# Eleven prefetched adapter tiles in a row behind the thirteen in place, the convolution's working memory released in two parts, and the first chunk's remaining rows begun an adapter sooner

## Chip, cores and metric

The kernel runs on one core of a Trainium2 chip. The metric is the device time of one execution in microseconds (us). The kernel before was run three times: 2236.38, 2232.4 and 2238.17, median 2236.38. The profiled execution took 2235.61, with a span of 2234.0 from the first to the last profiled instruction, so 1.6 us lie around the span.

## What is computed

The reference takes `x` of shape (32, 64, 1024): 32 samples of 64 rows. Four layers follow, each added to its input:

```python
x = x + _L0(x, ...)   # a state-space kernel K(64 rows x 1024), convolved with each row, plus D*x, masked by length
x = x + _L1(x, ids1, w1)   # w1[ids1[b]]: one 1024 x 1024 float32 matrix for each sample
x = x + _L2(x, ids2, w2)   # the same with another table and other ids
x = x + _L3(x, ...)   # gated feed-forward 1024 -> 2752 -> 1024, silu(gate) * up, with rank-16 adapters by sample
```

Everything is float32. L1 and L2 are the "adapters" here: each of the 32 samples needs a matrix of 4 MB of its own in each of the two layers, which is read from device memory for that sample alone.

## The kernel before

**Chunks.** The samples are handled in four chunks (`NCK`) of eight (`BC`). The convolution (`convolution`, called at L289) is computed for all chunks at once; the first chunk's result goes into `xs[0]` and the others' into the device buffer `cd`. Then chunk 0 goes through its 16 adapters (two layers by eight samples) and its feed-forward; the adapters of a later chunk are taken between pieces of the feed-forward of the chunk before it.

**An adapter's tiles.** A matrix is cut into eight tiles of 128 x 1024 float32 (512 KB, `KT` = 8). `adapter(layer, b)` (L252) takes tile after tile from the iterator `stream` and multiplies; `adapter_part` (L229) does one of the two halves (`s` = 0, 1) of the sample's 64 rows. When the eight tiles are through, VectorE (DVE) transposes the PSUM bank into the tile `y` (L263) and adds it to `x` (L265). The 128 tiles of chunk 0 are numbered k = 0 to 127 here, in the order in which TensorE (PE) needs them; `layers` (L155) gives the order of the adapters.

**Where tiles lie.** SyncE's queue (SP) issues all their loads, in the program's order. Nine places rotate (`wpool`, `ROTATING` = 9): a load into one waits until PE has read the tile that lies there. Besides there are places that hold one tile each, loaded while the convolution runs ("own" places, list `early`): 16 in `epool`, four in the half of `xpool` that chunk 1 will use, five ("late") where the convolution's tables lay, nine ("last") where its transfers lay. That makes 34; `own` (L184) says which k lie in them: 2, 5, 8, ... 101, every third. Before the adapters begin, 34 own tiles and the first nine others (k = 0, 1, 3, 4, 6, 7, 9, 10, 12) are on their way. `fetch(n)` issues the next n of these 43 loads in the order of k, at points written out by hand: L2072, L2021 (`MID`), L2074, then two a period, then `LATE` at L1997 and the rest at L1982.

**What the convolution frees, and when.** `g0` lives until `first.close()`, `gb` (transfers `uf`, `hk`, state of even groups, small tiles) until `filling.close()` at L1980, `s1` until `making.close()`. The last of the eight groups (`NG_`) is only multiplied with its taps (`direct`) after the carried part of the group before it; `filling.close()` stands behind both, so the nine loads into "last" wait for the last `direct`.

**Ahead.** While the convolution's last two groups run, PE does the half s = 0 of the first 13 tiles (`first_sides` L240: all eight of the first adapter, `SECOND_` = 5 of the second) in pieces (`ahead_`). When `xs[0]` is complete, the other half of these 13 follows, and then tile k = 13.

**From the adapters into the feed-forward.** After 12 adapters (`OWN_ENDS`) `first.close()` frees all own places and `g0`, and the pools of the feed-forward (`hpool`, `gpool`, `apool`, `qpool`) take their memory. Then the steps stand in this order (L1224 to L1262): `begin_rest(0)` (the product of one half of the chunk's rows with a weight tile `wr`, which takes a rotating place, L351); the loads of two feed-forward weights (`first_weight`, into `wf0_first` and `act_first`); adapter 13; a part of the feed-forward's moving sums; `begin_rest(1)`; adapter 14; tables of the low-rank part by GpSimd (POOL); `begin_rest(2)`; `begin_products(0)` with the two loaded weights; adapter 15; `begin_products(1)`; adapter 16. `wr0` keeps its rotating place until the feed-forward has used its second half.

**y.** Until `first.close()`, `y` lies in a pool of its own (`ypool`, 2 KB by partition); afterwards in `gpool`.

Of the kernel before, what the change touches and what calls it, by code (L numbers as in the profile page):

```python
# [9 lines left out]
F32 = mybir.dt.float32  # L10
# [9 lines left out]
P = 128  # L20
B, H, L = 32, 64, 1024
NS = 64
KT = L // P
NCK = 4
# [7 lines left out]
MB = 4  # L32
MG = 2
NG = FM // MG
EARLY = 16
OWN_ENDS = 12
LATE = 5
LAST = 9
KS = 5
WARM = 20  # L40
FIRST_ = 11
SECOND_ = 5
MID = 6
ROTATING = 9
HA = 4
# [39 lines left out]
def kernel(  # L85
# [95 lines left out]

    own = {3 * i + 2 for i in range(len(early) + LATE + LAST)}  # L184
    held = {}

    def first_weights():
# [29 lines left out]
        for _ in range(n):  # L217
            next(before, None)

    def places(n):  # L220

        late = n == LATE
        name = "late" if late else "last"
        pool = first.enter_context(
            tc.tile_pool(name=name, bufs=1, side="right" if late else "left")
        )
        for i in range(n):
            early.append(pool.tile([P, L], F32, tag=f"{name}{i}", name=f"{name}{i}"))

# [56 lines left out]
                ALU.add,  # L286
            )

    convolution(tc, cst, consts, xt, xf, ssm, eye, lens, xs[0], cd, ps_tile, fetch, places, (row_ids, rows_now), first, first_sides())  # L289
    for _ in before:  # L290
        pass

# [33 lines left out]
    def take(c):  # L326
# [12 lines left out]

    ypool = [
        first.enter_context(tc.tile_pool(name="ypool", bufs=1, reuse_waits="tile"))
    ]

    def adapters(c):
        for layer, b in layers(c):
# [839 lines left out]
    def begin_rest(i):  # L1187
        wt, ps = rest_tile(i, "first")[0], ps_tile(f"pr{i}_first")
        rest_part(0, wt, ps, 0, TH)
        nc.scalar.copy((rest1, rest2[:, 0], rest2[:, 1])[i][:, :TH], ps[:, :TH])  # L1190
        return wt
# [38 lines left out]
        first_weight(m, 0)  # L1230
    xb, part = first_moving()
    next(layers0)
    part(0, 2)
    begin_rest(1)
    next(layers0)
    tables = [
        columns(ag, 0, KT, "g_0", behind=loads[-1]),
        columns(au, 0, KT, "u_0", ("cu", "lt")),
    ]
    begin_rest(2)  # L1240
    begin_products(0)
    next(layers0)
    part(2, 3)
# [20 lines left out]
def convolution(tc, cst, consts, xt, xf, ssm, eye, lens, x0, cd, ps_tile, fetch, places, rows_now, first, sides):  # L1264
# [12 lines left out]
    with ExitStack() as ctx:  # L1277
        ctx.enter_context(tc.manual_schedule(engines={DVE, ACT, POOL, SP}))
        g0 = first.enter_context(tc.tile_pool(name="g0", bufs=1))
        filling, making = ExitStack(), ExitStack()  # L1280
        gb = filling.enter_context(tc.tile_pool(name="gb", bufs=1))
        s1 = making.enter_context(tc.tile_pool(name="s1", bufs=1, side="right"))
        dram = ctx.enter_context(
            tc.tile_pool(name="kdram", bufs=1, space=bass.MemoryType.DRAM)
# [10 lines left out]
        def load_u(g):  # L1295
            for u in range(PAIRS[g] // 2):
                i = first_unit[g] + u
                ufs[i] = gb.tile([P, HA, NCK, KT * BC], F32, tag="uf", name=f"uf{i}", bufs=4)
                nc.sync.dma_start(ufs[i], xf[:, i * HA : (i + 1) * HA])

        load_u(0)
# [423 lines left out]
        def load_taps(g):  # L1725
            for u in range(PAIRS[g] // 2):
                i = first_unit[g] + u
                hks[i] = gb.tile([P, HA, P], F32, tag="hk", name=f"hk{i}", bufs=2)
                queue = nc.scalar if g == NG_ - 1 else nc.sync
                queue.dma_start(  # L1730
                    hks[i],
                    bass.AP(
                        tensor=kps.tensor,
                        offset=kps[i * HA : i * HA + 1, 1:2].offset,
                        ap=[[1, P], [KROW, HA], [1, P]],
                    ),
                )
# [211 lines left out]
        def period(g):  # L1949


            steps = scan(g + 1) if units(g + 1) else iter(())
            ma, mb = (products(g + 3, u) for u in range(2))
            copies = []

            def turn_next(u):
                copies.append(powers_turned(g + 2, u))

            def copy():
                copies.pop(0)()  # L1960

            first, second = taken(g, 0), taken(g, 1)
            events = [(0, lambda: carried(g, 0))]
            if not units(g + 1):
                for u in range(2):
                    carried(g, u, KS, KT - 1)
                ahead_(SECOND_)
                for c0, c1 in ((0, 1), (1, NCK)):
                    for u in range(2):
                        for f in taken(g, u, c0, c1):  # L1970
                            f()
                return
            if not units(g + 2):

                def ahead():
                    ahead_(3)
                    for u in range(2):
                        direct(g + 1, u)
                    ahead_(3)
                    filling.close()  # L1980
                    places(LAST)
                    fetch(99)  # L1982

                events += [
                    (3, lambda: carried(g, 1)),
                    (3, ahead),
                    *spread(4, (*first, *second)),
                    (3 * KS - 3, lambda: carried(g + 1, 0, 0, KS)),
                    (3 * KS - 3, lambda: carried(g + 1, 1, 0, KS)),
                ]  # L1990
            elif not units(g + 3):

                def close():
                    kernels(g + 2)
                    making.close()
                    places(LATE)
                    fetch(LATE)  # L1997

                events = [
                    (0, lambda: turn_next(0)),  # L2000
                    (0, copy),
                    *events,
                    *spread(1, adds.pop((g + 2, 1))),
                    (3, lambda: carried(g, 1)),
                    (3, close),
                    *spread(3, first[:2]),
                    (4, lambda: inputs(g + 2, 0)),
                    (5, first[2]),
                    (6, lambda: turn_next(1)),
                    (6, copy),  # L2010
                    *spread(6, second),
                    (9, lambda: direct(g + 1, 0)),
                    (9, lambda: inputs(g + 2, 1)),
                    (12, lambda: (direct(g + 1, 1), ahead_(2))),
                ]
            elif g:
                events = [
                    (0, lambda: turn_next(0)),
                    (0, copy),
                    *events,  # L2020
                    *spread(1, adds.pop((g + 2, 1))),  # L2021
                    (3, lambda: carried(g, 1)),
                    *spread(3, first[:2]),
                    (4, lambda: made(ma, 8)),
                    (4, lambda: inputs(g + 2, 0)),
                    (5, first[2]),
                    (6, lambda: turn_next(1)),
                    (6, lambda: made(ma, 3)),
                    (6, copy),
                    *spread(6, second),  # L2030
                    (9, lambda: direct(g + 1, 0)),
                    (9, lambda: made(ma)),
                    (9, lambda: inputs(g + 2, 1)),
                    (9, lambda: made(mb, 3)),
                    (9, lambda: kernels(g + 2)),
                    (10, lambda: adds[g + 3, 0][0]()),
                    (11, lambda: adds.pop((g + 3, 0))[1]()),
                    (12, lambda: made(mb)),
                    (12, lambda: direct(g + 1, 1)),
                ]  # L2040
            else:
                events += [
                    *spread(1, adds.pop((g + 2, 0))),
                    (3, lambda: turn_next(0)),
                    (3, copy),
                    (3, lambda: carried(g, 1)),
                    *spread(3, first[:2]),
                    (4, lambda: made(ma, 8)),
                    (4, lambda: inputs(g + 2, 0)),
                    (5, first[2]),  # L2050
                    *spread(6, adds.pop((g + 2, 1))),
                    (8, lambda: turn_next(1)),
                    (8, lambda: made(ma, 3)),
                    (8, copy),
                    *spread(8, second),
                    (10, lambda: direct(g + 1, 0)),
                    (10, lambda: made(ma)),
                    (10, lambda: inputs(g + 2, 1)),
                    (10, lambda: made(mb, 3)),
                    (10, lambda: kernels(g + 2)),  # L2060
                    (13, lambda: adds[g + 3, 0][0]()),
                    (14, lambda: adds.pop((g + 3, 0))[1]()),
                    (14, lambda: made(mb)),
                    (14, lambda: direct(g + 1, 1)),
                ]
            run(steps, events)
            if units(g + 3):
                load_u(g + 3)
            if units(g + 2):
                load_taps(g + 2)  # L2070

        fetch(FIRST_)  # L2072
        opening()
        fetch(4)  # L2074
        for g in range(NG_):
            period(g)
            if g < NG_ - 4:
                fetch(2)
        rows_now[1]()

# [168 lines left out]
```

## Time and profile before

| | us |
|---|---|
| median of three runs (2232.4 to 2238.17) | 2236.38 |
| the profiled execution | 2235.61 |
| its span | 2234.0 |
| PE busy | 2190.5 (98%) |
| DVE busy | 1369.6 (61%) |
| ACT, POOL busy | 424.2, 207.9 |
| convolution: PE's first matmul to the end of the 13 tiles' second half | 8.4 to 148.3 |
| PE's longest wait for a tile | 148.3 to 155.1 |
| rest of chunk 0's adapters and what is mixed in | 155.1 to 278.5 |
| feed-forward and the later chunks' adapters | 278.5 to 2234.0 |

A row of the profile's timeline of an engine gives the start of a stretch of like instructions, its length, the line of the code, the operands and the number of records, and in brackets how long the engine had been idle and what ended that. PE has two records for each matmul of the code, so a whole tile is 16 records and one half of its rows is 8; "x" at the end counts records. In the profile "pa" is an adapter's PSUM bank, "wa" a tile in a rotating place, and "early", "x_early", "late", "last" are tiles in own places.

### The profile page before, as it was taken

Reading aid. Unit: us, or ns where it says so; the run is one execution under the profiler, and the core shown is the slowest. Engines: PE = TensorE matmul, PEld = TensorE weight load, DVE = VectorE, ACT = ScalarE, POOL = GpSimd, SP = SyncE. Lnnn points to the kernel's source line nnn. Section 1 sums busy time; section 2 is a strip of 40 time slices with the busy share of each in tenths; the row PEclk is TensorE's granted clock in tenths of the full one; section 3 lists DMA queues with packets and bytes.
Section 4 is the critical chain, followed back from the end, with each engine's and each line's share of the span. In section 5 each row is a group of like instructions: output and inputs, shape, how many; then the busy total and the mean of one; then the engine's idle time right before and its main releaser. Section 6 shows DMA issues by size and latency. Waiting matters only on the chain.

```text
span 2234.0 us, 53648 instructions
## 1 busy us (share of the span) xinstructions
PE 2190.5 (98%) x21488; PEld 1811.1 (81%) x21488; DVE 1369.6 (61%) x2995; ACT 424.2 (19%) x1042; POOL 207.9 (9%) x328
## 2 busy tenths in 40 slices
PE   6889999999999999999999999999999999999999
PEld 5756687877787897888689897789678988899998
DVE  8961277675367766466346667466336666576575
ACT  6800121110011121121012212022002212121220
POOL 1010031111011211000000111000000011000000
PEclk9999999999999999999999999999999999999999
DMA  8789998899979558799979848799989938384671
GB/s 313 264 326 408 383 385 304 327 365 358 362 286 362 207 198 306 288 360 362 350 281 367 282 146 321 267 351 364 353 292 360 334 107 290 117 295 177 214 275 42
DMA packets 204683, 656.35 MB, mean 294 GB/s; under 512 B 24066, under 2 KB 40834, under 8 KB 203922
## 3 DMA queue, kind: packets, MB, share of 16 engines
q1 hardware_dynamic: 173122, 565.84, 69.6%
q0 software_dynamic: 23392, 76.07, 9.1%
q10 hardware_dynamic: 7920, 11.01, 1.4%
q8 instruction: 169, 2.77, 0.5%
q14 instruction: 80, 0.66, 0.1%
HBM read 585.66 MB, written 67.17 MB: 292 GB/s over the span
## 4 chain that ended last, share of the span: by engine, by line
PE 85%; DMA 6%; DVE 5%; issue 3%; POOL 0%; ACT 0%; SPq 0%; POOLq 0%; DVEq 0%; ACTq 0%
PE pq L720 30%; PE po L1130 24%; PE pa L234 16%; PE pf L614 6%; DMA wa<-in_w 4%; PE pr L359 3%; PE pe L481 2%; DVE xg L1338 1%; DMA sums<-kept 1%; PE pl_d L452 1%; DVE t L1338 1%; DVE tmp L1338 1%; PE pr_first L359 0%; DVE zs L1338 0%; DMA hk<-kp 0%
## 5 line engine op out<-in xcount | busy, mean ns | idle before, releaser
L234 PE MATMUL pa<-wa,x 128*32 128x256 f32 x7648 | 435.3, 380 | 12.7 <-DMA wa<-in_w 12.4
L720 PE MATMUL pq<-xd,wa 128*128 128x128 f32 x3360 | 414.6, 275 | 0.0
L720 PEld LDWEIGHTS pq<-xd,wa 128*128 128x128 f32 x3360 | 394.6, 192 | 0.1
L234 PEld LDWEIGHTS pa<-wa,x 128*32 128x32 f32 x7648 | 244.8, 110 | 184.4 <-DMA wa<-in_w 21.9
L720 PE MATMUL pq<-xd,wb 128*128 128x128 f32 x2520 | 323.7, 276 | 0.0
L720 PEld LDWEIGHTS pq<-xd,wb 128*128 128x128 f32 x2520 | 300.5, 192 | 3.6
L263 DVE STREAM_TRANSPOSE y<-pa 128x512 f32<-128x512 f32 x64 | 45.9, 717 | 275.8 <-PE pa L234 275.8
L1130 PE MATMUL po<-act,wd 128*128 128x256 f32 x640 | 168.6, 386 | 0.0
L1130 PE MATMUL po<-actd,s 128*128 128x256 f32 x640 | 164.2, 379 | 0.0
L1130 PE MATMUL po<-actd,wd 128*128 128x256 f32 x640 | 164.2, 379 | 0.0
L507 DVE TENSOR_TENSOR s<-wd 128x256 f32<-128x256 f32 x80 | 33.8, 422 | 176.5 <-PE po L1130 176.4
L1130 PEld LDWEIGHTS po<-act,wd 128*128 128x128 f32 x640 | 117.8, 190 | 29.3 <-issue 12.9
L378 POOL DMA_INDIRECT bgu<-in_bgu,rows x44 | 44.7, 1016 | 984.2 <-PE pe L481 827.3
L614 PE MATMUL pf<-xd,wf 128*128 128x256 f32 x576 | 135.5, 381 | 0.0
L1130 PEld LDWEIGHTS po<-actd,s 128*128 128x128 f32 x640 | 121.6, 190 | 16.5
L1130 PEld LDWEIGHTS po<-actd,wd 128*128 128x128 f32 x640 | 121.6, 190 | 16.5
L1162 ACT COPY uo<-po 128x256 f32<-128x256 f32 x48 | 17.9, 373 | 615.0 <-PE po L1130 599.3
L614 PEld LDWEIGHTS pf<-xd,wf 128*128 128x128 f32 x576 | 108.7, 190 | 15.5
L614 PE MATMUL pf<-xd,s 128*128 128x256 f32 x480 | 114.5, 382 | 1.4 <-DVE up L655 0.9
L744 ACT COPY u<-pq 128x256 f32<-128x256 f32 x120 | 41.5, 346 | 366.7 <-PE pq L720 307.3
L614 PEld LDWEIGHTS pf<-xd,s 128*128 128x128 f32 x480 | 90.2, 190 | 17.3 <-DVE up L655 2.8
L749 DVE TENSOR_TENSOR u<-u,u 128x256 f32<-128x256 f32 x120 | 46.5, 388 | 73.2 <-ACT u L746 72.7
(273 smaller groups left out, 2762.4 us busy)
## 6 DMA issues: line engine op xcount, KB each, us to landing
wa<-in_w SPq DMA_DIRECT2D x478, 512.0 KB
wa<-sums SPq DMA_DIRECT2D x210, 512.0 KB
wb<-parts SPq DMA_DIRECT2D x120, 384.0 KB
wd<-in_wd SPq DMA_DIRECT2D x80, 512.0 KB
wb<-in_wq SPq DMA_DIRECT2D x90, 384.0 KB
sums<-kept POOLq DMA_DIRECT2D x30, 1024.0 KB
wf<-in_wu SPq DMA_DIRECT2D x20, 512.0 KB
uf<-in_xf SPq DMA_DIRECT2D x16, 512.0 KB
```

The lines of the kernel that those rows point to most:

```text
L234: nc.tensor.matmul(acc[i * S : (i + 1) * S, s * 256 : (s + 1) * 256], xs[lo // TC][:, kt, lo % TC + s * S : lo % TC + (s + 1) * S], wt[:, ...
L263: nc.vector.transpose(y, acc)
L359: nc.tensor.matmul(ps[:, tokens], wt[:, kt, :], xs[c][:, kt, tokens], start=(kt == 0), stop=(kt == KT - 1),)
L378: nc.gpsimd.indirect_dma_start(out=t, out_offset=None, in_=table, in_offset=bass.IndirectOffsetOnAxis(ap=at_, axis=0),)
L481: nc.tensor.matmul(ps[:, at_ * 2 * H : (at_ + 1) * 2 * H], bt[pair(j), g], tms[table][pair(j)], start=(g == 0), stop=True, skip_group_chec ...
L507: nc.vector.tensor_add(s1, a21, a22)
L614: nc.tensor.matmul(ps, ws[j][:, kt, :], xb[j][:, kt, :], start=start and kt == 0, stop=kt == KH - 1, skip_group_check=True,)
L720: nc.tensor.matmul(ps[:, to * TQ : (to + 1) * TQ], w[i][:, k, :], xb[:, j, SLOT[i], k, :], start=start and k == 0 and to == 0, stop=k == K ...
L744: nc.scalar.copy(u, pa)
L749: nc.vector.tensor_add(u, v, u)
L1130: nc.tensor.matmul(pss[j], *term, start=(s0 == m0 and i == 0 and home[j] % 2 == 0), stop=(end and i == len(terms) - 1 and not late), skip_ ...
L1338: nc.vector.tensor_tensor(o, a, b, op)
```

## The change

Five things change.

1. The own places are 35 (17 + 4 + 5 "late" + 4 "mid" + 5 "last"), and hold other tiles: k = 2, 5, 8, 11, then 13 to 23 without a gap, then 25, 28, ... 82. So the first 24 tiles are all in place or on their way; between 24 and 82 every third is. `fetch(5)` stands where `fetch(4)` stood.
2. The convolution's pool `gb` is split: `ga` holds `uf` and `hk` (20 KB by partition), `gb` the rest. `gb` is closed first (`drawing.close()`), behind the carried part of the group before the last; four tiles "mid" are loaded into its place. `ga` closes where `gb` closed, and five tiles "last" follow.
3. `y` has no pool of its own: until `first.close()` it takes the tile `t` in `g0`.
4. `OWN_ENDS` is 11: `first.close()`, `begin_rest(0)` and the two weight loads stand an adapter earlier; `begin_rest(1)` and `begin_rest(2)` also move in front of the adapter that stood before them, so each comes an adapter sooner.
5. The memory for GpSimd's DMA descriptors is 2048 bytes in place of 4096 by partition.

```diff
-EARLY = 16
-OWN_ENDS = 12
+EARLY = 17
+OWN_ENDS = 11
 LATE = 5
-LAST = 9
+BETWEEN = 4
+LAST = 5
+FIRST_RUN, RUN = 13, 11
...
-    own = {3 * i + 2 for i in range(len(early) + LATE + LAST)}
+    stock = len(early) + LATE + BETWEEN + LAST
+    ks = [*range(2, FIRST_RUN, 3), *range(FIRST_RUN, FIRST_RUN + RUN)]
+    own = set(ks) | {FIRST_RUN + RUN + 1 + 3 * i for i in range(stock - len(ks))}
...
-    convolution(tc, cst, consts, ...)
+    g0 = convolution(tc, cst, consts, ...)
...
-    ypool = [
-        first.enter_context(tc.tile_pool(name="ypool", bufs=1, reuse_waits="tile"))
-    ]
+    ypool = [g0]
...
     next(layers0)
+    begin_rest(1)
+    next(layers0)
     part(0, 2)
-    begin_rest(1)
+    begin_rest(2)
     next(layers0)
     tables = [
...
     ]
-    begin_rest(2)
     begin_products(0)
...
-        filling, making = ExitStack(), ExitStack()
-        gb = filling.enter_context(tc.tile_pool(name="gb", bufs=1))
+        filling, drawing, making = ExitStack(), ExitStack(), ExitStack()
+        ga = filling.enter_context(tc.tile_pool(name="ga", bufs=1))
+        gb = drawing.enter_context(tc.tile_pool(name="gb", bufs=1))
...
                 def ahead():
+                    drawing.close()
+                    places(BETWEEN, "mid", "right")
+                    fetch(BETWEEN)
                     ahead_(3)
                     for u in range(2):
                         direct(g + 1, u)
                     ahead_(3)
                     filling.close()
-                    places(LAST)
+                    places(LAST, "last", "left")
                     fetch(99)
...
         opening()
-        fetch(4)
+        fetch(5)
...
-        dynamic_dma_scratch_size=4096,
+        dynamic_dma_scratch_size=2048,
```

(`uf` and `hk` are taken from `ga`; `places` takes a name and a side; `convolution` returns `g0`.)

More of the change, by code (lines that the diff above doesn't have):

```diff
@@ L218, in fetch, with places @@
             next(before, None)
[L220 to L226, printed above, removed]
+    def places(n, name, side):
+        pool = first.enter_context(tc.tile_pool(name=name, bufs=1, side=side))
         for i in range(n):
@@ L287, in rows_now @@
             )
-    convolution(tc, cst, consts, xt, xf, ssm, eye, lens, xs[0], cd, ps_tile, fetch, places, (row_ids, rows_now), first, first_sides())
+    g0 = convolution(tc, cst, consts, xt, xf, ssm, eye, lens, xs[0], cd, ps_tile, fetch, places, (row_ids, rows_now), first, first_sides())
     for _ in before:
@@ L1297, in load_u @@
                 i = first_unit[g] + u
-                ufs[i] = gb.tile([P, HA, NCK, KT * BC], F32, tag="uf", name=f"uf{i}", bufs=4)
+                ufs[i] = ga.tile([P, HA, NCK, KT * BC], F32, tag="uf", name=f"uf{i}", bufs=4)
                 nc.sync.dma_start(ufs[i], xf[:, i * HA : (i + 1) * HA])
@@ L1727, in load_taps @@
                 i = first_unit[g] + u
-                hks[i] = gb.tile([P, HA, P], F32, tag="hk", name=f"hk{i}", bufs=2)
+                hks[i] = ga.tile([P, HA, P], F32, tag="hk", name=f"hk{i}", bufs=2)
                 queue = nc.scalar if g == NG_ - 1 else nc.sync
@@ L1995, in close @@
                     making.close()
-                    places(LATE)
+                    places(LATE, "late", "right")
                     fetch(LATE)
@@ L2079, in convolution @@
         rows_now[1]()
+    return g0
 def _constants(np):
```

## The prediction

> **What bounds the kernel.** I read four views, in this order. The first is the busy time on the page: PE is the bound, and a change can win only where PE stands still or runs slowly.
>
> ```profile
> PE 2190.5 (98%) x21488; PEld 1811.1 (81%) x21488; DVE 1369.6 (61%) x2995; ACT 424.2 (19%) x1042; POOL 207.9 (9%) x328
> ```
>
> Of 2234.0 us, 43.5 are idle. The second view is PE's waits between 0 and 345 us, the stretch that the change touches (what was waited for, us in total, times, longest):
>
> ```profile
> PE pa L234 <- DMA wa<-in_w: 8.6, 6, 6.8
> PE py L1782 <- DMA hk<-kp: 1.8, 2, 0.9
> PE pr_first L359 <- DMA wr_first<-in_wr: 0.3, 1, 0.3
> ```
>
> The largest wait is one of 6.8 us for a streamed tile. The third view, PE's timeline, places it and the rows that my sums use:
>
> ```profile
> 147.66 0.61 PE L234 MATMUL pa<-wa,x 128*32 128x256 f32 x8
> 155.08 1.93 PE L234 MATMUL pa<-wa,x 128*32 128x256 f32 x16 [6.80 <-DMA wa<-in_w]
> 156.79 1.75 PE L234 MATMUL pa<-early,x 128*32 128x256 f32 x16
> 158.36 1.90 PE L234 MATMUL pa<-wa,x 128*32 128x256 f32 x32
> ...
> 182.20 1.07 PE L234 MATMUL pa<-early,x 128*32 128x256 f32 x16
> ...
> 218.46 1.07 PE L234 MATMUL pa<-last,x 128*32 128x256 f32 x16
> ...
> 221.05 1.07 PE L234 MATMUL pa<-last,x 128*32 128x256 f32 x16
> ...
> 230.46 3.72 PE L359 MATMUL pr_first<-x,wr_first 128*128 128x256 f32 x16
> ...
> 278.51 2.05 PE L359 MATMUL pr<-x,wr_first 128*128 128x128 f32 x16
> ```
>
> After the second halves of the 13 tiles, PE idles until k = 13 lands. The next rows are slow: groups of 16 records follow each other after 1.71 and 1.57 us, and later after 0.86. The fourth view is the windows (length, busy of PE, PEld, DVE, ACT, POOL with counts, then the granted PE clock, the DMA engines' share, GB/s):
>
> ```profile
> 120.00:140.00 20.00, 18.68 (x201) 14.09 (x199) 18.25 (x50) 1.06 (x2) 0.00 (x0) 1.00 0.78 274
> 140.00:160.00 20.00, 13.20 (x216) 7.38 (x218) 6.34 (x17) 0.00 (x0) 8.81 (x16) 0.83 1.03 396
> 180.00:200.00 20.00, 19.62 (x368) 13.83 (x364) 4.23 (x6) 0.00 (x0) 0.00 (x0) 1.00 1.02 408
> 240.00:260.00 20.00, 19.05 (x197) 12.69 (x190) 5.40 (x8) 3.42 (x6) 0.00 (x0) 1.00 1.02 405
> ```
>
> The transfers are full from 140 to 260 us (396 to 408 GB/s) and have room before (274). SP's timeline says why: it issues the nine "last" loads from 134.97 on and k = 13 at 144.11, behind them. The trace has one load landing each 1.27 us here (25 in 32.61 us, 1.30, between 229.79 and 262.40); a load alone takes 3.5 us from issue to landing (134.97 to 138.51, 261.90 to 265.43).
>
> [...]
>
> **The ceiling.** (a) The wait of 6.80. (b) The slow rows behind it: 1.71 + 1.57 against 2 x 0.865, that is 1.55 us; the clock is 0.83 in 140–160 and 1.00 before and after, so I take it as bought by the idle time. (c) Six small waits up to 253 us: 0.57, 0.38, 0.32, 0.28, 0.20, 0.30, in all 2.05. Together 10.4 us.
>
> **The row of own tiles (items 1, 2).** PE's second halves end at 148.1 as before. Now k = 13 to 23 lie ready: from 182.20 to 221.05 there are 45 tiles in 38.85 us, 0.863 each, so k = 24 is reached at 148.1 + 11 x 0.863 = 157.6. Its load can be issued at about 143: only five "last" loads stand ahead of it, because four ("mid") now go out when the carried products of the group before the last end (128.8), into room that lay idle. Loads at intervals of 1.27 from about 147 keep ahead of PE, which takes two streamed tiles in 2.59 us. So (a), (b) and the first two of (c) go. PE then takes k = 83 at 148.1 + 70 x 0.863 = 208.5; before it was 218.46. That is **10.0 us earlier**.
>
> **Where part of it is given back (items 3, 4).** The built order of the changed kernel shows a new wait. `wf0_first` lies over `t` of `g0`, which is now `y`, so its load waits for DVE's add of the 11th adapter (L265); before, it had only to wait for the convolution. It stands on SP between the loads of k = 90 and k = 91, and behind it are k = 91 to 127 and two `wr` tiles: 39 loads. Adapter 11 ends at 148.1 + 75 x 0.863 = 212.8; DVE then takes 0.72 + 0.69 (rows 717 and 692 ns) with gaps, about 214.5. `wf0_first` goes out at 214.6 and, with the queue drained meanwhile, lands at 218.1. SP stands from about 208 to 214.6, and the transfers are idle for about 4 us of that. PE is covered for a while: one rest product (3.65, from 230.46 and 253.70) and k = 88 to 90, to 212.8 + 3.65 + 2.6 = 219.05, when k = 91 lands (219.4). From there the transfers decide: 218.1 + 39 x 1.295 = 268.6, and 0.9 for the last tile, so PE is through at **269.5 to 270**. PE's own work would end at 212.8 + 3.65 + 5 x 7.04 + 2 x 3.65 + 2 x 3.5 = 266. Before: 278.5. The gain is 8.5; about 3.5 of what the row could give are lost to the bytes behind that wait. The bounds of this cost are 0 (PE at 266) and 6.6 + 3.5 = 10.1 (SP's standstill and a landing, nothing covered); I take 3.5, by the recurrence.
>
> [...]
>
> `wr0` keeps its rotating place an adapter sooner, so eight places instead of nine serve one adapter more; with transfers full, eight in flight are the most the trace shows, so I cost it at nothing; with that cover gone it costs one load, 1.3. The rest products only change places: 3.65 each, as before.
>
> **Convolution (items 1, 2).** One more tile, 1.28 us of transfers, goes out ahead of `hk` of the third pair of loads; PE already waits for `hk` there:
>
> ```profile
> 65.01 1.97 PE L1782 MATMUL py<-uf,hk 128*128 128x256 f32 x8 [0.94 <-DMA hk<-kp]
> 131.14 3.69 PE L1782 MATMUL py<-uf,hk 128*128 128x256 f32 x16 [0.82 <-DMA hk<-kp]
> ```
>
> The bounds are 0 (DVE's chain absorbs it) and 0.7; I take 0.3. DVE's and POOL's built orders are unchanged.
>
> **After the adapters.** The feed-forward follows with the same instructions. Its loads stand about 1 us closer to PE, since transfers and not PE end the adapters: 0 to 1, I take 0.2. Item 5 costs nothing as long as POOL's issues don't wait (rival C).
>
> **Sum.** 8.5 − 0.3 − 0.2 = 8.0. Against the profiled execution 2235.61 − 8.0 = 2227.6; the median of the runs is 0.77 above it (2236.38), so **2228.4**.
>
> **Rivals.**
> A. The block on SP costs more: PE runs out of tiles at k = 91, and later loads come out of step with PE's products, so that the transfers pause again for a place. Two or three loads of 1.3 us are then lost, 3 in all: 8.0 − 3 = 5 gained, from 3 to 6.7, 2231.4. Slower transfers behind the block are the same rival: 0.1 us more a load costs 3.9. For it: 25 loads in 32.61 us leave nothing to catch up with. Against: PE has 6.2 us of cover (3.65 + 2.6), and no stretch of the trace is slower than 1.30 a load. Chance 0.20, 0.02 of it for slower transfers. [...]
> B. Only bytes count: the transfers were full to 260 us, and just one more tile is loaded early and four are moved into idle time. 5 x 1.28 = 6.4 gained: 2230.0. For it: the 405 GB/s of the last window. Against: 260 to 268 us had room (238 GB/s in 260–265). Chance 0.10.
> C. Slower: item 5. If POOL's issue of a gather (`bgu`, L378, 44 of them) has to wait until descriptors before it are used up, it lands late. One issued at 289.42 landed at 302.9 and PE used it at 304.86, a slack of 2.0; the next landed at 319.25 and was used at 334. A delay by one issue-to-landing time (222.43 to 230.18, 7.75) costs 5.8 at the former and nothing at the latter. It decides from the third gather of the tight kind: 17.4 lost, 2245.8. Against: the trace has no POOL issue that shows more than its 1 us. Chance 0.06. [...]
> D. It does not do what it says: the wait moves from k = 13 to k = 24, whole, 2236. The built order has the mid loads ahead of the last `direct`, so 0.04.
>
> **Chances.** Forecast 0.60, range of its own 2224.0 to 2231 (below: the ceiling of 10.4 gives 2226.0, and 2 more for the spread of the runs, 2232.4 to 2238.17; above: `hk` and the later loads at their upper ends and 1.3 for the place, 2.5 more than taken). About 0.3% (6.7 us) is what a measurement of this kernel can tell from no change: faster lies below 2229.7. Of the forecast 0.48 lies there, with 0.03 of A and 0.04 of B: faster 0.55; same 0.12 + 0.17 + 0.06 + 0.03 = 0.38; slower 0.06 + 0.01. The range takes in A and B: 2224.0 to 2233.5.
>
> **What would show it.** Right: no wait of PE near 148, clock 1.00 in 140–160; four "mid" loads at about 129–132 and a DMA share near 1 in 130–140; the row of k = 83 ("last") at 208.5; SP waiting some 6 us for DVE's `x` before `wf_first`, and a dip of the transfers at 213–217; waits of PE for `wa` of about 0.4 each between 219 and 250; the `pr` row after the adapters at 270 and the same spacing behind it. Wrong: a wait at k = 24 (D), a wait of over 1 us at k = 91 (A), `hk` waits that add more than 0.7, or PE waiting for `bgu` (C).

## The result and the profile after

The changed kernel takes 2227.59 us (median of 7 runs, 2225.63 to 2230.71) against 2234.15 for the kernel before beside it (7 runs): ratio 0.997, interval 0.9961 to 0.9979, 0.3% faster. Measured again later, in 11 runs, it took 2230.57 against 2235.85: 0.9974, 0.9964 to 0.9983. The profiled execution took 2230.71 (span 2229.1). It is the slowest of its seven, 4.9 us below the profiled execution of before (2235.61), so I read places in time from it and take the gain from the ratio.

Line numbers after are lower by 1 to 3 (L234 is now L233, L359 is L356). The changed kernel's PE timeline, at the places of the lines of before:

```profile
147.94 0.61 PE L233 MATMUL pa<-wa,x 128*32 128x256 f32 x8
148.38 9.68 PE L233 MATMUL pa<-early,x 128*32 128x256 f32 x176
157.87 1.05 PE L233 MATMUL pa<-wa,x 128*32 128x256 f32 x16
...
207.94 1.05 PE L233 MATMUL pa<-last,x 128*32 128x256 f32 x16
208.81 4.50 PE L233 MATMUL pa<-wa,x 128*32 128x256 f32 x80
213.24 3.72 PE L356 MATMUL pr_first<-x,wr_first 128*128 128x256 f32 x16
...
220.76 1.07 PE L233 MATMUL pa<-wa,x 128*32 128x256 f32 x16 [1.07 <-DMA wa<-in_w]
...
224.53 1.07 PE L233 MATMUL pa<-wa,x 128*32 128x256 f32 x16 [1.30 <-DMA wa<-in_w]
...
250.57 1.07 PE L233 MATMUL pa<-wa,x 128*32 128x256 f32 x16 [0.29 <-DMA wa<-in_w]
...
272.96 2.05 PE L356 MATMUL pr<-x,wr_first 128*128 128x128 f32 x16
```

Eleven own tiles (176 records) follow the second halves at once; no wait, no slow rows. k = 83 (a streamed tile now, the first of the 80 records at 208.81) begins 9.65 us sooner than before. But the adapters end at 272.96 instead of 278.51, only **5.55** sooner. The rest was given back between 219 and 251, in waits for tiles. PE's waits between 0 and 345 us:

```profile
PE py L1797 <- DVE xg L1337: 6.6, 7, 1.6
PE pa L233 <- DMA wa<-in_w: 3.8, 8, 1.3
PE pv L1682 <- DMA uf<-in_xf: 1.2, 1, 1.2
```

Six waits for streamed tiles (8.6 us, one of them 6.8) have become eight (3.8 us, the longest 1.3); the wait for `hk` at 65 us has become one for `uf`. The windows show the transfers (last two columns: their share and GB/s):

```profile
130.00:140.00 10.00, 9.65 (x116) 7.48 (x104) 8.87 (x26) 0.00 (x0) 0.00 (x0) 1.00 0.98 333
...
160.00:170.00 10.00, 10.00 (x192) 6.02 (x188) 1.41 (x2) 0.00 (x0) 0.00 (x0) 1.00 0.94 356
210.00:220.00 10.00, 9.69 (x128) 6.12 (x119) 1.41 (x2) 2.26 (x3) 0.00 (x0) 1.00 0.94 351
```

Before, the same three stretches had 188, 401 and 410 GB/s:

```profile
130.00:140.00 10.00, 9.18 (x110) 7.44 (x102) 8.63 (x25) 0.00 (x0) 0.00 (x0) 1.00 0.56 188
160.00:170.00 10.00, 9.43 (x178) 5.03 (x170) 2.29 (x4) 0.00 (x0) 0.00 (x0) 1.00 1.02 401
210.00:220.00 10.00, 10.00 (x192) 7.23 (x185) 2.09 (x3) 0.00 (x0) 0.00 (x0) 1.00 1.03 410
```

The "mid" tiles fill 130 to 140; two holes are new, at 160 and at 210.

### The profile page after: what moved, and what is told of

Read it like the earlier page. It is cut to its first block, busy times and chain, and to the rows that moved or that the text cites. A ratio compares the mean times of both kernels' runs of the same rounds, so it can differ in the third digit from the quotient of the medians.

```text
span 2229.1 us, 53636 instructions
## 1 busy us (share of the span) xinstructions
PE 2190.1 (98%) x21488; PEld 1806.0 (81%) x21488; DVE 1370.6 (61%) x2995; ACT 423.8 (19%) x1042; POOL 207.3 (9%) x328
## 4 chain that ended last, share of the span: by engine, by line
PE 86%; DVE 6%; DMA 5%; issue 3%; POOL 0%; ACT 0%; SPq 0%; POOLq 0%; DVEq 0%; ACTq 0%
PE pq L717 29%; PE po L1127 24%; PE pa L233 17%; PE pf L611 7%; PE pr L356 3%; DMA wa<-in_w 3%; PE pe L478 2%; DVE xg L1337 1%; DVE t L1337 1%; DMA sums<-kept 1%; PE pl_d L449 1%; DVE tmp L1337 1%; DMA wr_first<-in_wr 1%; PE pr_first L356 0%; DVE zs L1337 0%
## 5 line engine op out<-in xcount | busy, mean ns | idle before, releaser
L233 PE MATMUL pa<-wa,x 128*32 128x256 f32 x7632 | 431.7, 380 | 9.0 <-DMA wa<-in_w 9.0
L233 PEld LDWEIGHTS pa<-wa,x 128*32 128x32 f32 x7632 | 240.6, 110 | 183.4 <-DMA wa<-in_w 17.7
```

The source lines that it names most:

```text
L233: nc.tensor.matmul(acc[i * S : (i + 1) * S, s * 256 : (s + 1) * 256], xs[lo // TC][:, kt, lo % TC + s * S : lo % TC + (s + 1) * S], wt[:, ...
```

## The experiments

Two theories were set against each other. **IDLE** is the forecast's: PE's 6.8 us of idle time and the slow clock behind it are the loss, the row removes them, and SP's standstill gives some back. **BYTES** is the forecast's rival B, sharpened: from about 135 to 250 us the transfers decide, and only loads taken out of that stretch count. The end of the adapters (start of the `pr` row, 278.51 before, 272.96 after) is the finest scale, since a time's median has an interval of some 2 us. Each end is that of one execution, though, and the ends of the convolution in these executions differ by up to 2 us.

**The row alone**, on the kernel before.

```diff
-    own = {3 * i + 2 for i in range(len(early) + LATE + LAST)}
+    stock = len(early) + LATE + LAST
+    ks = [*range(2, 13, 3), *range(13, 24)]
+    own = set(ks) | {25 + 3 * i for i in range(stock - len(ks))}
```

> The kernel before with the row of own tiles alone: the same 34 places, but they hold k = 2, 5, 8, 11, 13 to 23, 25, 28, ... 79; nothing else is changed. Two theories. IDLE (the forecast's): what counts is PE's 6.8 us of waiting for k = 13 and the 1.55 us of slow clock behind it, so the row alone gives most of the gain: no long wait, PE through with chunk 0's adapters at about 270.5 instead of 278.5, some 8 us faster than before. BYTES: from about 135 to 250 us the transfers are full, so only loads taken out of that stretch count, and the row takes none out: the wait at 148 goes, but it comes back in small waits for tiles until about 253, PE is through with the adapters at 277.5 to 278.5, and the time is that of before within 1 us.

Measured: 2236.53, ratio 1.0004 (0.9995 to 1.0013). Its waits up to 345 us and its timeline:

```profile
PE pa L236 <- DMA wa<-in_w: 4.9, 20, 0.8
```

```profile
207.06 1.05 PE L236 MATMUL pa<-last,x 128*32 128x256 f32 x16
...
279.75 2.05 PE L361 MATMUL pr<-x,wr_first 128*128 128x128 f32 x16
```

The wait at 148 is gone (longest 0.8), and PE is early for a while: the row at 207.06 is k = 79, which the kernel before reached at about 215.0 (218.46 less 4 x 0.863). All of it comes back: there are 20 small waits (4.9 us), all from 211 us on, where streamed tiles in a row start 1.28 us apart (211.21, 212.49, 213.76, ...), the pace of the loads, instead of 0.863. The end is 1.2 us later than before. There is no block on SP here. IDLE falls: **the 6.8 us of waiting was where the lack of bytes showed, not what caused it.**

**The split alone**, and **row and split**, on the kernel before.

```diff
+        ga = filling.enter_context(tc.tile_pool(name="ga", bufs=1))
+        gb = drawing.enter_context(tc.tile_pool(name="gb", bufs=1))
...
                 def ahead():
+                    drawing.close()
+                    places(BETWEEN, "mid", "right")
+                    fetch(BETWEEN)
```

> The kernel before with the split of the convolution's pool alone: four mid and five last places in place of nine last, own tiles every third as before. BYTES: four loads leave the full stretch, 4 x 1.27 = 5.1 us: PE through with the adapters at 273.4, time 5 us below before. IDLE: the load of k = 13 stands behind five loads instead of nine, so it lands about 5 us sooner and the wait of 6.8 shrinks to about 1.7; the gain is about the same 5 to 6 us. Here both give nearly one number; the run is the partner of the next two.

Measured: 2231.87, ratio 0.9986 (0.9977 to 0.9995), adapters' end 274.79, 3.7 sooner instead of the expected 5.1.

> The kernel before with the row and the split, without the earlier rest products, the 17th place, the new place of y and the smaller descriptor memory. IDLE: no long wait and no block on SP: 8.5 to 10 us faster than before, PE through with the adapters at 268.5 to 270. BYTES: as the split alone, 5.1 us faster, PE through at 273.4, with small waits of PE for tiles between 200 and 253 us.

Measured: 2231.36, ratio 0.9987 (0.9978 to 0.9996), the same as the split alone; end 276.68, which is neither the 268.5 to 270 of IDLE nor the 273.4 of BYTES. The convolution ran late in this execution (its last `py`-`xg` row starts at 127.27, the split's at 125.42), so the two ends can't be set against each other to the microsecond. The split's windows:

```profile
130.00:140.00 10.00, 9.64 (x112) 7.80 (x112) 8.84 (x25) 0.00 (x0) 0.00 (x0) 1.00 1.00 352
140.00:150.00 10.00, 8.15 (x148) 4.44 (x152) 5.46 (x16) 0.00 (x0) 4.98 (x9) 1.00 0.98 348
```

352 instead of 188 in the first is 1.64 MB more, 4.05 us at 405 GB/s; 348 instead of 390 in the second gives 1.0 back. Net 3.0 of the 3.7. PE waits in it 0.53, 1.49 and 0.68 us for streamed tiles at 149 to 155, and is no worse for it than with the row.

**The changed kernel without the block on SP.** In the changed kernel SP waits for DVE's add, between 195 and 225 us:

```profile
SPq L535 <- DVE x L264: 6.2, 1, 6.2
```

This edit moves the two loads behind another adapter:

```diff
-    for m in range(MG):
-        first_weight(m, 0)
     xb, part = first_moving()
     next(layers0)
+    for m in range(MG):
+        first_weight(m, 0)
     begin_rest(1)
```

> The changed kernel with one edit: the two loads into wf0_first and act_first stand behind the 12th adapter's loads instead of ahead of them, so SP reaches the load that waits for DVE's add of the 11th adapter when that add is long done. IDLE: the standstill of SP cost 3.5 to 4.5 us; without it PE is through with the adapters at 268.5 to 269.5 instead of 272.96, some 4 us faster than the changed kernel. BYTES: eight loads were in flight when SP stood, and the queue ran dry only for a moment; what is lost is the restart of an empty queue (after it the first three loads landed 2.30, 1.40 and 2.37 us apart instead of 1.27), 2.3 us in all: PE through at 270.6, some 2.3 us faster than the changed kernel.

Measured: 2228.69, 0.9967 (0.9957 to 0.9976); end 272.33, 0.63 sooner than the changed kernel. The hole at 210–220 is filled (409 for 351 GB/s, 0.58 MB, 1.4 us), but 130–140 (315 for 333) and 160–170 (340 for 356) carried 0.34 MB less in this execution. So the standstill costs 1.4 by the bytes, 0.6 by the end, and not 3.5: both numbers expected were too high, and by the ratio (0.997 for the changed kernel) no gain is to be seen.

**Item 4 undone.** `OWN_ENDS` is 12 again, and `begin_rest(1)` and `begin_rest(2)` stand where they stood.

> The changed kernel with item 4 undone: own places freed after 12 adapters, and the rest products where the kernel before has them. TAIL: transfers decide until k = 111 and wr2 have landed; what PE does after that decides the end, and with the rest products late that is 24.8 us (before: 253.70 to 278.51) and with them early 22.4 (changed kernel: 250.57 to 272.96). So item 4 is worth 2.4: PE through with the adapters at 275.4, 2.4 us slower than the changed kernel. Rival BLOCK: item 4 brings nothing of its own, it only puts SP's standstill for wf0_first an adapter sooner: 273 within 0.5.

Measured: 2231.48, 0.9986 (0.9978 to 0.9995); end 275.66, 2.70 later than the changed kernel. TAIL holds: behind the last wait for a load PE works 24.8 us (250.85 to 275.66) instead of 22.4. Up to k = 111, three `wr` tiles and two weights the loads decide, and from there on PE's work; a rest product ahead of that point costs its load (1.27), behind it PE's 3.65, and 2.4 is the difference. The hole at SP's block is here too, ten us later and deeper (292 GB/s in 220–230).

**One place fewer**: `EARLY` 16, `fetch(4)`.

> The changed kernel with 16 places in epool instead of 17, so 34 in all (the last own tile is k = 79) and one more tile is streamed. BYTES: one load of 512 KB more in the full stretch, 1.27 us: PE through with the adapters at 274.2, time 1.3 above the changed kernel, less the 0.25 us that the extra load costs in the convolution. IDLE: the tile is loaded while PE works, no long wait arises: 272.7 to 273.

Measured: 2229.72, 0.998 (0.9971 to 0.9988); end 275.30, 2.34 later than the changed kernel. BYTES (274.2) is the nearer, and still 1.1 too early. One load is 1.27 of the 2.34. The rest is a deeper hole (327 and 373 GB/s in 210–230 for 351 and 403).

**Own places spread.**

```diff
-    ks = [*range(2, FIRST_RUN, 3), *range(FIRST_RUN, FIRST_RUN + RUN)]
-    own = set(ks) | {FIRST_RUN + RUN + 1 + 3 * i for i in range(stock - len(ks))}
+    ks = [*range(2, 13, 3), 13, 14, 15, 17, 18, 20, 21, 23, 24, 26]
+    own = set(ks) | {27 + 3 * i for i in range(stock - len(ks))}
```

> The changed kernel with the 35 own places spread: k = 2, 5, 8, 11, 13, 14, 15, 17, 18, 20, 21, 23, 24, 26, 27, 30, ... 87, so that a streamed tile is taken after two or three own ones and its place comes free. BYTES: the row of eleven kept the rotating places occupied (no streamed tile taken from 148.4 to 157.9) and the transfers fell to 356 GB/s in 160-170; spread, they stay near 405, 0.49 MB or 1.2 us more: PE through with the adapters at 271.7 instead of 272.96. IDLE: the row is what keeps PE from waiting; without it PE waits for streamed tiles between 148 and 165, and the end is the same or later, 273 to 274.

Measured: 2225.75, 0.9962 (0.9949 to 0.9976); end 272.07, 0.89 sooner, though the convolution ended 0.7 later in this execution. Near the expected 271.7, but not by the expected way: 160–170 rose only from 356 to 368. The hole at 210–220 closed:

```profile
160.00:170.00 10.00, 10.00 (x192) 6.01 (x188) 1.70 (x3) 0.00 (x0) 0.00 (x0) 1.00 0.98 368
210.00:220.00 10.00, 10.00 (x136) 6.59 (x132) 1.41 (x2) 2.23 (x3) 1.03 (x1) 1.00 1.03 406
```

SP still stands for DVE's add until 215.6 (4.7 us), but with four loads in flight, the last of which lands at 220.5, and `wf_first` 1.28 behind it. In this run the standstill cost nothing: the four loads in flight outlasted it, and 210–220 carried 406 GB/s.

**Three edits**: the spread, the later weight loads, and `begin_products(1)` right behind `begin_products(0)`.

> Three edits on the changed kernel: the spread own places, the two weight loads behind the 12th adapter's loads, and both feed-forward products ahead of the 15th adapter. BYTES and TAIL together: 1.2 for the transfers at 160, 1.3 for those at 215, and up to 1.0 for PE's work taken out of the end (16 tiles then end it, at one load per 1.27 us): PE through with the adapters at 269.5 to 270.5, some 3 us faster than the changed kernel. If the places and not the bytes bound it: 272 to 273.

Measured: 2228.94, 0.9977 (0.9967 to 0.9986); end 274.45. A miss, by 4 to 5 us; the last sentence's direction holds, at an even later end. The windows:

```profile
250.00:260.00 10.00, 10.00 (x84) 7.57 (x88) 1.41 (x2) 1.49 (x4) 0.00 (x0) 1.00 0.90 357
260.00:270.00 10.00, 9.61 (x176) 5.15 (x168) 4.62 (x9) 2.36 (x3) 1.49 (x3) 1.00 0.95 344
```

Both products together are 7 us (250.96 to 258) in which PE reads no streamed tile. No place comes free: SP waits 7.0 us for PE, the transfers sink, and the last adapter waits five times. In this run the 7 us of work without loads outlasted the loads in flight, and 250–260 and 260–270 carried 357 and 344 GB/s where the spread alone has 391 and 406. Not all of the miss is this: the convolution ended 0.7 later than with the spread alone, and one rest product took 1.7 us longer (last section).

**The two last stores into `cd` on GpSimd's queue**, on the spread and on the changed kernel.

```diff
-                    queue = nc.scalar if g >= NG_ - 3 else nc.sync
+                    late = nc.gpsimd if g == NG_ - 1 else nc.scalar
+                    queue = late if g >= NG_ - 3 else nc.sync
```

> The spread own places and one more edit: the last two stores into cd are issued by GpSimd's queue instead of ScalarE's. LANE: in the kernels so far SP stands at 148 to 155 and again to 160 for these stores (waits of up to 5.9 us for cd), since each of its loads waits for the one of SP and ACT eight back; the transfers fall to 356 to 368 GB/s in 160-170 for that reason. With the stores on another queue they stay near 405, 0.4 MB or 1 us more, PE through with the adapters 1 us sooner than with the spread alone (271 where the convolution ends at the same time). Rival PLACE: the dip comes from rotating places that PE has not read yet, and the wait for cd only hides it: SP then stands for PE at the same time, no change.

Measured: 2226.49 (5 runs), 0.9957 (0.9943 to 0.997); end 271.92, against 272.07. The convolution's last `py`-`xg` row starts 0.9 sooner here (125.41 for 126.30), so no gain of the edit is shown.

> The changed kernel with that edit alone (the last two stores into cd by GpSimd's queue). LANE: transfers near 405 GB/s in 160-170 instead of 356, PE through at 272 instead of 272.96. PLACE: in this kernel the row of eleven own tiles keeps the rotating places occupied until 157.9, so SP stands for PE and the dip stays; the end does not move.

Measured: 2228.77, 0.9971 (0.9961 to 0.9981); end 273.32, against 272.96. SP's waits from 140 to 170, first the changed kernel, then this one:

```profile
SPq L181 <- DMA cd<-tmp: 13.7, 3, 5.9
SPq L181 <- PE pa L233: 5.3, 8, 1.4
```

```profile
SPq L181 <- PE pa L233: 16.1, 12, 8.1
SPq L181 <- DMA cd<-tmp: 3.7, 1, 3.7
```

PLACE: one wait takes the other's place. The dip shrinks (389 GB/s), but 140–150 and 150–160 carry less (381 and 393 GB/s for 401 and 401), and the end stays. What each of the two waits would cost without the other is not shown.

**Item 5 alone.**

> The kernel before with item 5 alone: 2048 instead of 4096 bytes by partition for GpSimd's descriptors. Forecast: nothing, the time of before within 1 us, and POOL's gathers of about 1.0 us each. Rival C: gathers that wait for their descriptors, more than 6 us slower.

Measured: 2235.46, 0.9996 (0.9987 to 1.0006); end 278.53; the gathers' row, which for the kernel before says 44.7 and 1016:

```profile
L378 POOL DMA_INDIRECT bgu<-in_bgu,rows x44 | 45.6, 1037 | 981.0 <-PE pe L481 823.5 <-PE pe_rest L481 90.4 <-PE pa L234 64.4
```

Nothing measurable, as forecast.

**The changed kernel again.**

> The changed kernel itself once more, beside the two others on the same chip: 2227.6 within 1.5 us, 0.3% below before, and about 1 to 2 us above the spread.

Measured: 2230.57, 0.9974, end 272.76. The time is a miss, 3 us above the one expected; but the kernel before was 1.7 higher beside it too, and the ratio (0.3%) is as expected. The spread with the stores moved was 4 us faster beside it, though its interval (up to 0.997) still meets that of this kernel (from 0.9964).

**The bytes add up.** In MB, what the transfers carried from 120 to 250 us (13 windows of 10 us); the end worked out as 278.51, less the MB over 50.00 at 0.405 MB per us, less 1.3 where a 17th place is loaded before 120 us, less 2.4 where item 4 is in (PE's part behind the last of these loads: 253.70 to 278.51 before, 250.57 to 272.96 after):

| kernel | MB | end worked out | end measured |
|---|---|---|---|
| before | 50.00 | 278.5 | 278.51 |
| row alone | 49.68 | 279.3 | 279.75 |
| split alone | 51.36 | 275.2 | 274.79 |
| row and split | 50.78 | 276.6 | 276.68 |
| changed | 50.71 | 273.1 | 272.96 |
| changed, again | 50.62 | 273.3 | 272.76 |
| without the block | 50.77 | 272.9 | 272.33 |
| item 4 undone | 50.42 | 276.2 | 275.66 |
| one place fewer | 50.01 | 276.1 | 275.30 |
| spread | 51.24 | 271.7 | 272.07 |
| spread, stores moved | 50.84 | 272.7 | 271.92 |
| stores moved | 50.55 | 273.5 | 273.32 |
| item 5 alone | 49.97 | 278.6 | 278.53 |

All within 0.9 us (the three edits are left out: their end has another order). The ends span 7.8 us, and no term for PE's long wait or its clock is needed. The changed kernel's 5.55 is thus 1.8 (0.71 MB) + 1.3 + 2.4. This is a sum made when the ends were known: 2.4 comes from the kernel before and the changed one, and the runs that test the two terms, item 4 undone (2.70 later than the changed kernel) and one place fewer (2.34), carry fewer bytes too. It tells how late the loads are, not why: a stretch also carried fewer bytes when SP stood (351 GB/s in 210–220 of the changed kernel) or no place was free (357 in 250–260 of the three edits).

## Why the prediction was right, point by point

The time was forecast well (2228.4 against 2227.59, gain 8.0 against 6.6, and against 5.3 when measured again); the mechanism was not. That the number came near is luck: 10.0 us stand in it for the row and the split, which by themselves brought about 3 (ratio 0.9987), and nothing for the earlier rest products, which are worth 2.4.

- **The row (10.0 us).** As a place in time it was right: no wait, clock 1.00, k = 83 at 208.81 for 208.5. As a gain it was wrong. The step that failed is "the ceiling", which took the wait, its slow clock and the small waits as independent losses to be removed. The row alone gains nothing (1.0004), the row and the split about 3 us (0.9987), with the wait gone in both. The forecast's own reading of the fourth view, transfers full from 140 to 260, spoke against it; rival B drew that conclusion. (The sign named for k = 83 has a slip: the "last" row, at 207.94, is k = 82.)
- **The block on SP (3.5).** SP waited 6.2 us for DVE's `x` (forecast 6), `wf_first` went out at 214.85 (214.6) and landed at 218.42 (218.1). Then the forecast let loads land every 1.295 at once. The first three landed 2.30, 1.40 and 2.37 apart, 2.2 more than at that rate. The trace of before had the price: behind the load issued at 261.90, which the forecast read as one that lands alone though two others were still in flight, the next three landed 2.46, 1.59 and 1.86 apart. That is most of the 3 us between the end forecast (269.5 to 270) and measured. Taking the block away gives less back, 0.6 at the end and 1.4 by the bytes of 210–220; why not the whole 2.2 is open. The rest of the 3.5 that the forecast laid to the block was the lack of bytes: row and split, which has no such block (407 GB/s in 210–220), ends late too (276.68).
- **Item 4.** It was costed as a loss, its rest products as only changing places. Undone, it moves the end by 2.7, of which 2.4 is PE's work behind the last load.
- **The convolution (0.3).** In the changed kernel's execution the last `py`-`xg` row starts at 125.95 for 125.59, a cost of 0.36. Over all executions with 17 places it starts between 125.4 and 127.1, with 16 at 125.4 to 125.6 and once at 127.3 (row and split). What the 17th place costs there is lost in a spread of 2 us.
- **The feed-forward (0.2), item 5 (0).** From the `pr` row to the end of the span: 1956.1 after, 1955.5 before, 0.6; the descriptor memory costs nothing measurable (item 5 alone: ratio 0.9996, 0.9987 to 1.0006).
- **The rivals.** B had the cause. Its 6.4 counted the right loads, but no hole and nothing for item 4, two errors of 1 to 3 us that cancel in part; so did those of the forecast. A's signature, a wait of over 1 us at k = 91, is there (1.07), and so is about its price: the end is 3 us later than forecast. Its reason is not: the transfers don't pause again for a place, the lateness lies in the three landings after the block, and behind them loads land 1.25 to 1.33 apart up to 246 us. Nor are there the slower transfers that A also allowed: behind the block the changed kernel shows 409 and 408 GB/s (230–240, 240–250), and from 170 to 210 us every execution shows 404 to 412.

## What to carry to other kernels

Before a wait is costed as a gain, ask whether the resource behind it is full from there to the next point where nobody waits for it. Here it was: moving the wait alone brought nothing (ratio 1.0004), while bytes that left the full stretch (the split, 3.7 us sooner at the adapters' end) and work that needs none and moved ahead of its end (item 4, 2.7) counted. Add up the bytes of the stretch in both kernels: that sum, with two terms for what lies outside it, gave the end of thirteen executions to within a microsecond, after the fact. Loads in flight hid a standstill of their issuer here when there were three or more (0.0 to 0.3 us lost behind it), and did not when there were two or one (2.3 to 3.4 us).

## What was not expected of the hardware

- Restart of a queue that has run down: with two loads still in flight, the first new one took 3.5 us and the next three landed 2.1 to 2.3 us in all later than at 1.27 apart, in both kernels. In these runs the loss goes with how many are in flight when SP goes on with `wf_first`. Counted from the last landing before it to the fourth from there, the loss was 0.0 and 0.3 us with four and five in flight (the spread, without and with the stores moved), 0.1 with three (stores moved), 2.3 with two (the changed kernel, both times), 2.9 and 3.4 with one (item 4 undone, one place fewer).
- Waits for tiles do not slow the clock alike: 1.49 us (split) and 2.86 us (without the block) left it at 1.00, while behind 2.23 us (three edits) a rest product took 5.38 us instead of 3.69 (clock 0.92 and 0.91 in 220–230 and 230–240) and behind 2.29 (item 4 undone) the clock was 0.69 in 230–240. What decides is not shown by these runs.
